# A weight product of 128 matmuls rebuilt from 28 half products, with two steps of the order moved

## The chip, the cores and the metric

The kernel runs on one core of one Trainium2 chip. The metric is the device time of a whole execution in microseconds (us). Over three runs the kernel before took 1076.21 us in the median, 1075.88 to 1081.52 us. In this text PE is the matrix engine (TensorE), DVE is VectorE, ACT is ScalarE, POOL is GpSimd, and SP is the engine whose queue issues most plain transfers. "L709" is line 709 of the kernel before; lines of the changed kernel are named as such.

## The reference

There are N = 2708 nodes with D = 1024 features and a sparse 0/1 matrix `adj` of N x N. Everything is float32. Two layers follow each other:

```python
q, k, v = x @ Wq.T + bq, x @ Wk.T + bk, x @ Wv.T + bv
z = (q @ k.T) / sqrt(D) * adj
z = where(z == 0, -10000, z)
x = layernorm(x + relu(softmax(z, axis=1) @ v))     # layer 0
x = layernorm(x + adj @ (x @ W1) + b1)              # layer 1
```

A row of `adj` holds few ones, and more of them in the low rows. So only the scores of those neighbours are needed.

## The kernel before, in words

**Sizes.** P = 128 rows make a block; there are NB = 22 blocks. The 1024 features are DC = 8 chunks of 128, or NH = 2 halves of 512. One float32 matmul with 512 columns shows up in the profile as two records.

**Opening.** Wq and Wk are loaded and turned on PE (`flip_w`, L263; copied out of PSUM by ACT and DVE in turn at L266 and L268) into `wq_o` (four tiles) and `wk_o` (one tile). From these the kernel forms the score matrix M = Wq^T Wk (L701 to L711), so that a score is x M x^T. M has 8 row blocks (`i`) by 2 halves (`h`), 16 outputs of 128 x 512, each a sum over 8 chunks: 128 matmuls. Each output is copied from its PSUM bank by ACT (L711) into a quarter tile `m_q`. Four PSUM banks (`p_o`) serve this.

**Lists of neighbours.** Between the outputs of M the program places `list_columns` (L226 to L247), one call for each of the 22 row blocks of `adj`: ACT counts the ones of the row in two passes (L231, L232), DVE finds the positions by six `max_index` over parts of the row (L235) and sorts them into 24 keys with some small operations (L237 to L245). The row block comes by a transfer on SP's queue into one of three tiles `a`; POOL writes six small marks into the tile ahead of it (L213). Sixteen lists (EARLY) are spread evenly over M. Once nine lists are placed, `sort_begin(0)` (L605 on) makes class flags of the first eight blocks on DVE (`hot`, L626); once eleven are, `sort_end(0)` counts them with two matmuls on PE (L632, L634), DVE turns the counts into places (L638 on) and POOL scatters eight records (L659). The rows are so ordered by their number of neighbours. A scheduler lays the instructions of each engine into one queue, so where the program places a call only influences where it stands in the queue.

**Block products.** `y_block(b)` (L371 to L388) forms y = x M for one block: 16 matmuls into two banks (L378), DVE adds a row (`add`, L320) and the block goes to DRAM. The loop at L757 runs the first eight (FAMILY) of these with the last six lists between them, and calls `next(deal)` after blocks 0, 1, 3, 4 and 5 (L767). `deal` is the generator `deal_hub` (L462 on), which spreads the rows with the most neighbours ("hub": up to 80 keys in each quarter row) over 128 partitions. Its steps in turn: gather the record and the four quarter rows (L494); search 80 keys by ten pairs of 677-wide DVE operations (L503, L505) and count them (`n_q`, L508); a matmul of the counts on PE (L519) with small DVE work; place the shares with eleven small DVE operations (L531 on); a transpose. The next step, eleven gathers `found`, stands in the loop of later blocks. `row_constants` (L746) is one 1024-wide DVE operation for each block.

**Attention.** The remaining blocks' products alternate with `attend` calls: POOL gathers a block's y rows (`yg`, L435) and neighbours (`g`, L441), DVE forms scores (L917) and weighted sums (L974, L1058). A credit, an estimate of time, decides how many calls go between two PE steps. The first `yg` reads the eight stored blocks of `y_block`. Then pairs of row blocks go through Wv with seven half products (`pair_products`, L322): a 2 x 2 block scheme that takes 7 products of half depth where 8 were needed, at the price of sums and differences on DVE.

**Layer 1.** `units` (L1290) gives ten pairs of row blocks in an order written by hand. For each pair POOL gathers neighbours (`sum_rows`, L1295) three units ahead, DVE sums them (L1310), `turn1` transposes the sums on PE one unit ahead of the products (`flip` L836; for block 0 `flip_shares`, L849, which also takes the hub's sums), `work1` is again seven half products. The hub's eleven gathers are placed when i == 3 (L1377). Slots to gather per block: block 0 has 15, the hub 11, block 6 has 3, blocks 5 and 11 have 4 each.

Of the kernel before, what the change touches and what calls it, by code (L numbers as in the profile page):

```python
# [9 lines left out]
F32 = mybir.dt.float32  # L10
# [5 lines left out]
ALU = mybir.AluOpType  # L16
# [4 lines left out]
P = 128  # L21
# [3 lines left out]
HALF = 512  # L25
HUB = 32
HUB_SLOTS = 11
HUB_KEYS = 80
FAMILY = 8
# [9 lines left out]
EARLY = 16  # L39
# [41 lines left out]
def sparse_part(ctx, tc, x, xT, adj, wqT, wkT, wvT, bq, bk, bv, w1, b1, out):  # L81
    nc = tc.nc
    N, D = x.shape
    DC = D // P
    NH = D // HALF
    scale = 1.0 / math.sqrt(D)
    NB = (N + P - 1) // P
    assert NB == len(SLOTS)
    rows = [min(P, N - b * P) for b in range(NB)]
# [21 lines left out]
    with es:  # L111
# [6 lines left out]
        p_o = es.enter_context(tc.tile_pool(name="p_o", bufs=4, space=PSUM))  # L118
# [4 lines left out]
        wb = tc.alloc_tile_pool(name="wb", bufs=1)  # L123
# [102 lines left out]
        def list_columns():  # L226
            b = listed[0]
            listed[0] += 1
            n, a = rows[b], loaded[b]

            nc.scalar.activation(junk[:n], a[:n], AF.Sign, accum_out=cnt[:n, b:b + 1])  # L231
            nc.scalar.activation(junk[:n], a[:n], AF.Relu, scale=-1.0, accum_out=neg[:n, b:b + 1])  # L232
            at = lists.tile([P, RANGES, 8], U16, name="at_a", bufs=2)
            for i in range(RANGES):
                nc.vector.max_index(at[:n, i], ones[:n, :8], a[:n, cuts[i] + 8 * i:cuts[i + 1] + 8 * i + 8])  # L235
            there = lists.tile([P, RANGES, 8], F32, name="there", bufs=2)
            nc.vector.tensor_tensor(there[:n], at[:n], ends[:n], op=ALU.is_lt)  # L237
# [12 lines left out]
        bcast_rows(bq_bc, bq_sb)  # L250
        bcast_rows(bk_bc, bk_sb)
        wq_o = [wv_pool.tile([P, DC, 2 * P], F32, name=f"wq_o{q}", tag=f"v{q}") for q in range(4)]
        wk_o = wb.tile([P, DC, D], F32, name="wk_o")

        def flip_w(dst, src):

            n = 0
            for c in range(DC):
                for g in range(DC // 4):
                    tr = p_tr.tile([P, 4, P], F32, name="tr")  # L260
                    for k in range(4):
                        o = g * 4 + k
                        nc.tensor.transpose(tr[:, k, :], src(c)[:, o * P:(o + 1) * P], ident)  # L263
                    to = dst(c)[:, g * 4:g * 4 + 4, :]
# [6 lines left out]
        flip_w(lambda c: wq_o[c // 2][:, :, c % 2 * P:(c % 2 + 1) * P], lambda c: wq_i[c // 2][:, c % 2, :])  # L271
        flip_w(lambda c: wk_o[:, :, c * P:(c + 1) * P], lambda c: wk_i[:, c, :])
        load_adj()
        load_adj()
        for c in range(DC):
# [5 lines left out]
        nc.vector.scalar_tensor_tensor(junk[:, :DC], bq_sb, scale, bk_sb, op0=ALU.mult,  # L281
                                       op1=ALU.mult, accum_out=bqk)
        wk_pool.release()
        xa = tc.alloc_tile_pool(name="xa", bufs=2, side="right", reuse_waits="tile")
        xs = xa.tile([P, DC, NB], F32, name="xs", bufs=1)
        junka = xa.tile([P, P], F32, name="junka", bufs=1)
        x_last = xa.tile([P, DC, HUB], F32, name="x_last", bufs=1)
        nc.vector.memset(x_last, 0.0)
        xts = []

        def load_x():
            b = len(xts)
            if b == NB - 1:
                return
            r0, n = b * P, rows[b]
            xt = xa.tile([P, DC, P], F32, name="xt", bufs=3)
            nc.sync.dma_start(out=xt, in_=xT[:, r0:r0 + n].rearrange("(c p) n -> p c n", p=P))
            xts.append(xt)

        load_adj()  # L300
        for _ in range(3):
            load_x()
        yos = [xa.tile([P, D], F32, name=f"yo{k}", bufs=1) for k in range(3)]
# [396 lines left out]

        m_q = [[wm_pool.tile([P, DC // 2, HALF], F32, name=f"m{i}{j}", tag=f"m{2 * i + j}") for j in range(NH)]  # L701
               for i in range(2)]
        done = 0
        for i in range(DC):
            for h in range(NH):
                hs = slice(h * HALF, (h + 1) * HALF)
                po = p_o.tile([P, HALF], F32, name="po")
                for o in range(DC):
                    nc.tensor.matmul(po, wq_o[i // 2][:, o, i % 2 * P:(i % 2 + 1) * P], wk_o[:, o, hs],  # L709
                                     start=(o == 0), stop=(o == DC - 1))  # L710
                nc.scalar.copy(m_q[i // 4][h][:, i % 4], po)  # L711
                while done < EARLY * (i * NH + h + 1) // (DC * NH):
                    list_columns()
                    done += 1
                    if done == FAMILY + 1:
                        sort_begin(0)
                if not sorted_ and done > FAMILY + 2:
                    records_out(*sort_end(0), 0, FAMILY)
                    sorted_.append(0)
# [37 lines left out]
        for b in range(FAMILY):  # L757
            while done < min(NB, EARLY + 2 * (b + 1)):
                list_columns()
                done += 1  # L760
            y_block(b)
            if b == 1:
                bcast_rows(u_bc, u_col)
            if b == 2:
                load_last()
            if b in (0, 1, 3, 4, 5):
                next(deal)  # L767
            row_constants(len(c_ready))
# [518 lines left out]
        bias1 = hp.tile([P, D], F32, name="bias1", tag="bias")  # L1287
        nc.sync.dma_start(out=bias1, in_=b1.to_broadcast([P, D]))

        units = [(19, 18), (17, 16), (15, 1), (14, 2), (7, 8), (9, 3), (4, 10), (6, 0), (5, 11), (12, 13)]  # L1290
        assert sorted(last + [b for unit in units for b in unit]) == list(range(NB))
        last_norm = applied[-1]
        firsts = []
# [408 lines left out]
```

## Time and profile before

| what | value |
|---|---|
| median of the three runs | 1076.21 us |
| the profiled execution's own time | 1077.36 us |
| its span, first to last instruction | 1075.6 us |
| mean granted PE clock | 0.961 |
| POOL busy | 472.9 us (44%) |
| ACT busy | 432.8 us (40%) |
| bytes moved | 228.80 MB, mean 213 GB/s |

The profile was taken on another execution than the three timed runs; its span is 1.8 us below its own time. "Busy" is time in which an engine executes; a line of the timeline gives start, length, engine, source line, operation, tiles with shapes, how many records it joins, and in brackets the idle time ahead of it and what released it.

### The profile page before, as it was taken

What the parts mean: (1) busy time and instruction counts of PE and PEld (TensorE: products, weight loads), DVE (VectorE), ACT (ScalarE), POOL (GpSimd) and SP (SyncE); (2) the same over time, 40 slices, a digit from 0 to 9 for tenths busy, and PEclk for the clock granted to TensorE, in tenths of its full rate; (3) what the DMA queues carried; (4) which work ended last, traced back from release to release, by engine and by line L of the source; (5) the groups of instructions that cost most, each with busy time, mean ns of one, the idle gap of its engine ahead of it and who ended that gap; (6) DMA issues with size and microseconds to landing.
All of it is one profiled execution on the core that took longest, in us unless ns stands there. A gap on an engine that the chain in (4) does not pass through costs nothing.

```text
span 1075.6 us, 10690 instructions
## 1 busy us (share of the span) xinstructions
PE 981.1 (91%) x2761; PEld 464.8 (43%) x2761; DVE 821.1 (76%) x2039; ACT 432.8 (40%) x902; POOL 472.9 (44%) x520
## 2 busy tenths in 40 slices
PE   8999999598999998889999999997699899769993
PEld 6444444243444443345454444443344344334441
DVE  8999698980588987997999999544668879667332
ACT  4599896042223322332433443323222432244421
POOL 0000500025267665343665663211778678867300
PEclk9999999799999998999999999999799999979997
DMA  9698858968587767545456875226778698888601
GB/s 356 186 294 242 254 161 280 317 211 233 153 274 242 232 220 219 155 143 170 142 175 216 290 237 187 82 75 236 191 284 240 177 323 320 261 227 290 135 39 42
DMA packets 105782, 228.80 MB, mean 213 GB/s; under 512 B 22500, under 2 KB 49900, under 8 KB 105710
## 3 DMA queue, kind: packets, MB, share of 16 engines
q0 software_dynamic: 48192, 147.52, 43.8%
q1 hardware_dynamic: 57518, 80.50, 23.8%
q8 instruction: 23, 0.38, 0.1%
q14 instruction: 49, 0.40, 0.1%
HBM read 217.60 MB, written 33.68 MB: 234 GB/s over the span
## 4 chain that ended last, share of the span: by engine, by line
PE 30%; DVE 18%; issue 16%; DMA 10%; POOL 8%; ACT 1%; SPq 0%; POOLq 0%; DVEq 0%; ACTq 0%
PE po L306 24%; POOL g L441 5%; PE po L378 4%; DVE junkv L917 3%; DVE r L1310 3%; DMA g<-in_x_dram,tabs 2%; DVE r L974 2%; DMA g<-x_d,tabs 2%; DMA g<-x_d,tab_h 2%; PE tr L836 1%; DVE yo L320 1%; DVE r L1058 1%; POOL yg L435 1%; POOL xr L435 1%; DMA out_dram<-t,tabs 1%
## 5 line engine op out<-in xcount | busy, mean ns | idle before, releaser
L378 PE MATMUL po<-m,xt 128*128 128x512 f32 x672 | 297.3, 603 | 8.3 <-DVE yo L320 4.8
L378 PEld LDWEIGHTS po<-m,xt 128*128 128x128 f32 x672 | 129.4, 194 | 171.7 <-issue 163.3
L306 PE MATMUL po<-t,s_all 128*128 128x512 f32 x320 | 146.5, 601 | 9.8 <-DVE xr L320 8.4
L917 DVE SCALAR_TENSOR_TENSOR junkv<-yg,g 128x1024 uint8<-128x1024 f32 x108 | 131.7, 1220 | 26.6 <-DMA g<-in_x_dram,tabs 11.9
L441 POOL DMA_INDIRECT g<-in_x_dram,tabs x84 | 108.0, 1286 | 57.2 <-DVE r L974 16.7
L1310 DVE SCALAR_TENSOR_TENSOR r<-g,valid,r 128x1024 f32<-128x1024 f32 x77 | 98.2, 1282 | 20.9 <-DMA g<-x_d,tabs 10.2
L709 PE MATMUL po<-wk_o,wq_o 128*128 128x512 f32 x256 | 110.5, 592 | 0.0
L306 PEld LDWEIGHTS po<-t,s_all 128*128 128x128 f32 x320 | 60.6, 192 | 90.6 <-issue 71.2
L441 POOL DMA_INDIRECT g<-x_d,tabs x66 | 77.8, 1179 | 25.1 <-issue 16.5
L424 ACT ACTIVATE junka<-xt 128x128 f32<-128x128 f32 x168 | 51.7, 308 | 78.9 <-PE po L378 61.7
L235 DVE FIND_INDEX8 at_a<-ones,a 128x8 uint16<-128x83 f32 (+3 forms) x132 | 82.7, 630 | 0.0
L879 ACT ACTIVATE junks<-t,lnm 128x1024 uint8<-128x1024 f32 (+1 forms) x40 | 45.9, 1148 | 89.7 <-DVE lnm L877 89.4
L974 DVE SCALAR_TENSOR_TENSOR r<-g,pr,r 128x1024 f32<-128x1024 f32 x64 | 81.7, 1280 | 0.2
L306 PE MATMUL po<-wv,s_all 128*128 128x512 f32 x160 | 74.5, 610 | 4.0 <-DVE s_all L1097 4.0
L837 ACT COPY rT<-tr 128x512 f32<-128x512 f32 x76 | 41.0, 590 | 91.2 <-PE tr L836 89.3
L709 PEld LDWEIGHTS po<-wk_o,wq_o 128*128 128x128 f32 x256 | 48.3, 190 | 59.3 <-issue 58.6
L306 PE MATMUL po<-t,rT 128*128 128x512 f32 x160 | 73.7, 603 | 0.3 <-DVE t L320 0.3
L306 PE MATMUL po<-w,rT 128*128 128x512 f32 x160 | 72.8, 600 | 0.0
L306 PE MATMUL po<-w,s_all 128*128 128x512 f32 x160 | 72.1, 592 | 0.0
L306 PE MATMUL po<-wv,rT 128*128 128x512 f32 x160 | 70.5, 592 | 0.0
L892 ACT ACTIVATE t<-t,nmr,rstd 128x1024 f32<-128x1024 f32 (+1 forms) x40 | 49.1, 1237 | 41.7 <-DVE nmr L891 33.5
L231 ACT ACTIVATE junk<-a 128x2756 uint8<-128x2756 f32 (+1 forms) x22 | 55.0, 2500 | 9.5 <-DMA a<-in_adj_dram 4.2
(354 smaller groups left out, 1393.9 us busy)
## 6 DMA issues: line engine op xcount, KB each, us to landing
xt<-in_xT_dram SPq DMA_DIRECT2D x21, 512.0 KB
y_d<-yo SPq DMA_DIRECT2D x21, 512.0 KB
a<-in_x_dram SPq DMA_DIRECT2D x21, 512.0 KB
a<-in_adj_dram SPq DMA_DIRECT2D x21, 413.5 KB
a<-in_adj_dram SPq DMA_DIRECT2D x21, 338.5 KB
a<-in_adj_dram SPq DMA_DIRECT2D x21, 263.5 KB
wq_i<-in_wqT_dram SPq DMA_DIRECT2D x8, 512.0 KB
wk_i<-in_wkT_dram SPq DMA_DIRECT2D x8, 512.0 KB
```

The costliest lines, as they stand in the source:

```text
L231: nc.scalar.activation(junk[:n], a[:n], AF.Sign, accum_out=cnt[:n, b:b + 1])
L235: nc.vector.max_index(at[:n, i], ones[:n, :8], a[:n, cuts[i] + 8 * i:cuts[i + 1] + 8 * i + 8])
L306: put = nc.tensor.matmul(acc, a[:, k], w[:, k], start=start and k == 0, stop=stop and k == DC // 2 - 1, skip_group_check=True)
L378: put = nc.tensor.matmul(po, xts[b][:, c, :], m_q[c // 4][h][:, c % 4], start=(c == 0), stop=(c == DC - 1))
L424: put = nc.scalar.activation(junka[:, :xt.shape[2]], xt[:, c, :], AF.Copy, accum_out=xs[:, c, b:b + 1])
L441: nc.gpsimd.indirect_dma_start(out=dst[:n], out_offset=None, in_=src, in_offset=bass.IndirectOffsetOnAxis(ap=at, axis=0), bounds_check=N - ...
L709: nc.tensor.matmul(po, wq_o[i // 2][:, o, i % 2 * P:(i % 2 + 1) * P], wk_o[:, o, hs], start=(o == 0), stop=(o == DC - 1))
L879: nc.scalar.activation(junks[:n], t[:n], AF.Square, bias=nm[:n], accum_out=vs[:n])
L892: applied.append(nc.scalar.activation(t[:n], t[:n], AF.Identity, bias=nmr[:n], scale=rstd[:n]))
L917: nc.vector.scalar_tensor_tensor(junkv[:n], yg[:n, :D], scale, xg[:n], op0=ALU.mult, op1=ALU.mult, accum_out=s)
L974: nc.vector.scalar_tensor_tensor(r[:n], xg[j][:n], pr[:n, j:j + 1], r[:n], op0=ALU.mult, op1=ALU.add)
L1310: put = nc.vector.scalar_tensor_tensor(r[:n], xg[:n], ok[:n, j:j + 1], r[:n], op0=ALU.mult, op1=ALU.add)
```

## The change

Three parts. **M by pairs of row blocks.** Row blocks c and c + 4 of M are formed together by seven half products of 4 matmuls each (28 half products for the four pairs, so 112 matmuls). `wk_o` becomes four quarter tiles. DVE forms four 128 x 2048 differences of quarters and adds 12 PSUM outputs of 128 x 512 into `m_q`; POOL forms 16 sums and differences of 128 x 512 of `wq_o`. ACT still copies 16 outputs. A bank `pa` is copied in the middle of its sum and then summed on. The other products use the three banks of the transposes (`spare_bank`). The loads of x and the pool `xa` move behind M, since `xa` takes the memory that `mt` holds during M. **Hub.** `next(deal)` is called after blocks 0, 1, 4, 5, 6 instead of 0, 1, 3, 4, 5. **Layer 1.** The pair (5, 11) is now eighth and (6, 0) ninth; the hub's gathers are placed at i == 4.

```diff
-        wk_o = wb.tile([P, DC, D], F32, name="wk_o")
+        wk_o = [[wb.tile([P, DC // 2, HALF], F32, name=f"wk_o{g}{h}", bufs=1) for h in range(NH)] for g in range(DC // 4)]
...
-        xa = tc.alloc_tile_pool(name="xa", bufs=2, side="right", reuse_waits="tile")
...
+        mt = tc.alloc_tile_pool(name="mt", bufs=1, side="right", reuse_waits="tile")
...
-        done = 0
-        for i in range(DC):
-            for h in range(NH):
-                hs = slice(h * HALF, (h + 1) * HALF)
-                po = p_o.tile([P, HALF], F32, name="po")
-                for o in range(DC):
-                    nc.tensor.matmul(po, wq_o[i // 2][:, o, i % 2 * P:(i % 2 + 1) * P], wk_o[:, o, hs],
-                                     start=(o == 0), stop=(o == DC - 1))
-                nc.scalar.copy(m_q[i // 4][h][:, i % 4], po)
-                while done < EARLY * (i * NH + h + 1) // (DC * NH):
...
+        done, worked = 0, 0
+
+        def product_of_m(acc, a, w, start, stop):
+            nonlocal done, worked
+            half_products(acc, a, w, start, stop)
+            worked += 1
+            while done < EARLY * worked // (7 * DC // 2):
+                list_columns()
+                done += 1
+                if done == FAMILY + 1:
+                    sort_begin(0)
+            if not sorted_ and done > FAMILY + 2:
+                records_out(*sort_end(0), 0, FAMILY)
+                sorted_.append(0)
...
+        (w11, w12), (w21, w22) = wk_o
+        A = [[(wq_of(i)[:, :DC // 2], wq_of(i)[:, DC // 2:]) for i in (c, c + DC // 2)] for c in half]
...
+        nc.vector.tensor_sub(w12, w12, w11)
+        nc.vector.tensor_sub(m_t2, w22, w12)
+        for c in half:
+            nc.gpsimd.tensor_tensor(s_a[c], A[c][1][0], A[c][1][1], op=ALU.add)
+            nc.gpsimd.tensor_tensor(s_b[c], s_a[c], A[c][0][0], op=ALU.subtract)
+        pa = [bank() for c in half]
+        for c in half:
+            product_of_m(pa[c], A[c][0][0], w11, True, False)
+            nc.scalar.copy(m_q[0][0][:, c], pa[c])
+        for c in half:
+            pb = spare_bank()
+            product_of_m(pb, A[c][0][1], w21, True, True)
+            add(m_q[0][0][:, c], pb, m_q[0][0][:, c])
+        nc.vector.tensor_sub(w11, m_t2, w11)
+        nc.vector.tensor_sub(w21, w21, m_t2)
+        for c in half:
+            product_of_m(pa[c], s_b[c], m_t2, False, False)
+            nc.scalar.copy(m_q[0][1][:, c], pa[c])
+            nc.gpsimd.tensor_tensor(s_b[c], A[c][0][1], s_b[c], op=ALU.subtract)
+        for two in (half[:2], half[2:]):
+            pc = {}
+            for c in two:
+                pc[c] = spare_bank()
+                product_of_m(pc[c], s_a[c], w12, True, False)
+                nc.scalar.copy(m_q[1][1][:, c], pc[c])
+                nc.gpsimd.tensor_tensor(s_a[c], A[c][0][0], A[c][1][0], op=ALU.subtract)
+            for c in two:
+                product_of_m(pc[c], s_b[c], w22, False, True)
+                add(m_q[0][1][:, c], pc[c], m_q[0][1][:, c])
+            for c in two:
+                product_of_m(pa[c], s_a[c], w11, False, False)
+                add(m_q[1][1][:, c], pa[c], m_q[1][1][:, c])
+        for c in half:
+            product_of_m(pa[c], A[c][1][1], w21, False, True)
+            nc.scalar.copy(m_q[1][0][:, c], pa[c])
+        mt.release()
+        xa = tc.alloc_tile_pool(name="xa", bufs=2, side="right", reuse_waits="tile")
...
-            if b in (0, 1, 3, 4, 5):
+            if b in (0, 1, 4, 5, 6):
                 next(deal)
...
-        units = [(19, 18), (17, 16), (15, 1), (14, 2), (7, 8), (9, 3), (4, 10), (6, 0), (5, 11), (12, 13)]
+        units = [(19, 18), (17, 16), (15, 1), (14, 2), (7, 8), (9, 3), (4, 10), (5, 11), (6, 0), (12, 13)]
...
-            if i == 3:
+            if i == 4:
                 sum_rows("hub")
```

In the changed kernel's PE queue, as built, the two matmuls of the first sort stand behind 86 of the 112 matmuls of M; in the kernel before they stand behind 88 of 128. The matmul of `n_q` stands behind 80 matmuls of the block products (five blocks), in the kernel before behind 70.

More of the change, by code (lines that the diff above doesn't have):

```diff
@@ L263, in flip_w @@
                         nc.tensor.transpose(tr[:, k, :], src(c)[:, o * P:(o + 1) * P], ident)
-                    to = dst(c)[:, g * 4:g * 4 + 4, :]
+                    to = dst(c, g)
                     if n % 2:
@@ L269, in flip_w, with wq_of @@
                     n += 1
-        flip_w(lambda c: wq_o[c // 2][:, :, c % 2 * P:(c % 2 + 1) * P], lambda c: wq_i[c // 2][:, c % 2, :])
-        flip_w(lambda c: wk_o[:, :, c * P:(c + 1) * P], lambda c: wk_i[:, c, :])
+        def wq_of(i):
+            return wq_o[i // 2][:, :, i % 2 * P:(i % 2 + 1) * P]
+        flip_w(lambda c, g: wq_of(c)[:, g * 4:g * 4 + 4, :], lambda c: wq_i[c // 2][:, c % 2, :])
+        flip_w(lambda c, g: wk_o[g][c // 4][:, :, c % 4 * P:(c % 4 + 1) * P], lambda c: wk_i[:, c, :])
         load_adj()
@@ L283, in sparse_part @@
         wk_pool.release()
-        xa = tc.alloc_tile_pool(name="xa", bufs=2, side="right", reuse_waits="tile")
[L285 to L298, printed above, removed]
+        mt = tc.alloc_tile_pool(name="mt", bufs=1, side="right", reuse_waits="tile")
         load_adj()
-        for _ in range(3):
-            load_x()
-        yos = [xa.tile([P, D], F32, name=f"yo{k}", bufs=1) for k in range(3)]
         def half_products(acc, a, w, start=True, stop=True):
@@ L702, in sparse_part @@
                for i in range(2)]
-        done = 0
-        for i in range(DC):
-            for h in range(NH):
-                hs = slice(h * HALF, (h + 1) * HALF)
-                po = p_o.tile([P, HALF], F32, name="po")
-                for o in range(DC):
-                    nc.tensor.matmul(po, wq_o[i // 2][:, o, i % 2 * P:(i % 2 + 1) * P], wk_o[:, o, hs],
-                                     start=(o == 0), stop=(o == DC - 1))
-                nc.scalar.copy(m_q[i // 4][h][:, i % 4], po)
-                while done < EARLY * (i * NH + h + 1) // (DC * NH):
[L713 to L719, printed above, removed]
+        done, worked = 0, 0
@@ new lines, in product_of_m, with spare_bank @@
+        def product_of_m(acc, a, w, start, stop):
[10 more added lines that the diff above has]
+                sorted_.append(0)
+        def spare_bank():
+            return p_tr.tile([P, 4, P], F32, name="tr").rearrange("p a b -> p (a b)")
@@ new lines, in sparse_part @@
+        half = range(DC // 2)
+        (w11, w12), (w21, w22) = wk_o
+        A = [[(wq_of(i)[:, :DC // 2], wq_of(i)[:, DC // 2:]) for i in (c, c + DC // 2)] for c in half]
+        s_a, s_b = [[mt.tile([P, DC // 2, P], F32, name=f"{n}{c}") for c in half] for n in ("s_a", "s_b")]
+        m_t2 = mt.tile([P, DC // 2, HALF], F32, name="m_t2")
+        nc.vector.tensor_sub(w12, w12, w11)
[3 more added lines that the diff above has]
+            nc.gpsimd.tensor_tensor(s_b[c], s_a[c], A[c][0][0], op=ALU.subtract)
@@ new lines, in sparse_part, with load_x @@
+        for c in half:
[3 more added lines that the diff above has]
+        xa = tc.alloc_tile_pool(name="xa", bufs=2, side="right", reuse_waits="tile")
+        xs = xa.tile([P, DC, NB], F32, name="xs", bufs=1)
+        junka = xa.tile([P, P], F32, name="junka", bufs=1)
+        x_last = xa.tile([P, DC, HUB], F32, name="x_last", bufs=1)
+        nc.vector.memset(x_last, 0.0)
+        xts = []
+        def load_x():
+            b = len(xts)
+            if b == NB - 1:
+                return
+            r0, n = b * P, rows[b]
+            xt = xa.tile([P, DC, P], F32, name="xt", bufs=3)
+            nc.sync.dma_start(out=xt, in_=xT[:, r0:r0 + n].rearrange("(c p) n -> p c n", p=P))
+            xts.append(xt)
@@ L720, in sparse_part @@
+        for _ in range(3):
+            load_x()
+        yos = [xa.tile([P, D], F32, name=f"yo{k}", bufs=1) for k in range(3)]
         c_all = stat.tile([P, NB, YW - D], F32, name="c_all", bufs=1)
```

## The prediction

> **What bounds the kernel now.** I read the engine totals first, then a table of 20 us stretches, then the PE's timeline, then for each wait the timeline of the engine it waits for. The totals, and the group of M:
>
> ```profile
> PE 981.1 (91%) x2761; PEld 464.8 (43%) x2761; DVE 821.1 (76%) x2039; ACT 432.8 (40%) x902; POOL 472.9 (44%) x520
> L709 PE MATMUL po<-wk_o,wq_o 128*128 128x512 f32 x256 | 110.5, 592 | 0.0
> ```
>
> PE leads over the whole, but M is one stage. Its 256 records are 128 matmuls at 110.5/128 = 0.86 us each. The stage by stretches (stretch, sum, then busy PE, PEld, DVE, ACT, POOL, clock, DMA share, GB/s):
>
> ```profile
> 60.00:80.00 20.00, 20.00 (x48) 8.85 (x47) 19.73 (x89) 19.82 (x18) 0.83 (x18) 1.00 0.88 273
> 80.00:100.00 20.00, 20.00 (x48) 8.82 (x47) 19.80 (x117) 19.69 (x20) 1.10 (x24) 1.00 0.85 246
> 180.00:200.00 20.00, 18.42 (x43) 7.79 (x41) 20.00 (x41) 4.83 (x24) 0.00 (x0) 1.00 0.99 347
> ```
>
> PE, DVE and ACT are all full during M: the lists take DVE 4.8 us each and ACT two passes of 2.5 us each (5.3 us with their ends). From 180 us DVE alone is full. PE's timeline shows what follows:
>
> ```profile
> 101.35 0.42 PE L632 MATMUL mm<-hot,lower 128*128 128x152 f32 x2
> 101.86 34.50 PE L709 MATMUL po<-wk_o,wq_o 128*128 128x512 f32 x80
> 165.64 32.78 PE L378 MATMUL po<-m,xt 128*128 128x512 f32 x76
> 210.87 0.58 PE L519 MATMUL mm<-n_q,alike 128*128 128x1 f32 x2 [12.46 <-DVE junk_h L508]
> ```
>
> The sort's matmul has no wait: DVE had finished its `hot` at 98.2. The matmul of `n_q` waits 12.46 us for DVE's 80-key search, and the next 20 records take 11.39 us where 20 x 0.43 = 8.6 is usual, 2.8 more. On the other side stands block 7: POOL's next gather waits for its stored y.
>
> ```profile
> 277.93 0.94 POOL L435 DMA_INDIRECT yg<-y_d,tabs  x1 [17.77 <-issue]
> ```
>
> PE ends block 7 at 269.1, so y landed some 9 us later. Everything of the attention hangs on this; from 425 to 675 us DVE is about 97% busy, from 660 to 746 PE, with no slack that would swallow an earlier start. Layer 1 has one large wait:
>
> ```profile
> 951.41 0.74 PE L849 MATMUL tr<-to,r 128*128 128x96 f32 x2 [15.85 <-DVE r L1310]
> ```
>
> PE waits for block 0's sums, whose fifteen gathers stand late in POOL's queue:
>
> ```profile
> 921.88 0.99 POOL L441 DMA_INDIRECT g<-x_d,tab  x1 [0.30 <-issue]
> ...
> 943.35 0.99 POOL L441 DMA_INDIRECT g<-x_d,tab  x1 [0.30 <-issue]
> ```
>
> **What the Trainium skill says.** "TensorE: Matmul & The Clock Gate" (section "Architectural detail", queue depths) has ACT and DVE as strict FIFO; the queue orders below rest on this, and the trace agrees: the search on DVE runs in line with the 1.2 us row constants. Its Part 1 says that an idle PE falls to half clock; the 2.8 us lost after the 12.46 us wait agree, with clock 0.66 in that stretch. "GPSIMD Engine Reference" (section 3.1) gives 4497 ns on GpSimd for a float32 add of 2048 elements, 2293 on DVE; the DVE side agrees (2.28 us for the 128x2048 differences at L1196), the POOL side is shown by no row. "SBUF — State Buffer" (section "Who interferes with whom") says that a DVE operation with two SBUF inputs and a GpSimd operation that reads SBUF exclude each other; no row here shows it.
>
> **M on PE.** 16 matmuls fewer x 0.859 = 13.75 us. The half products keep their 512 columns, so the price of one stays. Against this PE now waits where a bank is copied by ACT before it is summed on: I take 2.4 us in all before the sort and 0.5 after it (bounds 0 and 6; an ACT pass ahead of a copy is 2.5 us long, but three to four banks are in turn).
>
> **M on DVE.** Four differences at 2.2 (the stride of those at L1200) and twelve PSUM adds at 0.61 (the stride of L320) make 16.1 us, in a stage where DVE is 99% full. Summing the durations of DVE's queue as built, `hot` comes at 105.3 us after; before, the same sum stood some 3.3 us ahead of the trace. Lists that start about 2.5 us later (the first difference stands ahead of list 1) make it about 111. PE reaches that matmul, behind 86 of 112, at 22.7 + 3.0 (transposes between) + 86 x 0.859 + 2.4 = 102. **So PE waits 9 us for the sort, where it had none**; behind it in PE's queue are the other 26 matmuls and all block products. They end at 111 + 0.8 + 22.3 + 0.5 = 134.6, before 136.2: of 13.75 us only 1.6 is left. After such a wait the clock may be down; I take 1.5 us of the 2.8 seen (bounds 0 and 2.8).
>
> **M on POOL.** 16 operations of 512 elements, at 4497/4 = 1.12 us each (an estimate from the skill's page): 18 us on an engine that is busy 1 us in 20 here. Eight come before their use; the other eight wait for a product, and the marks of the tiles for later lists stand behind them. I take nothing for that, bounded by rival C. The loads of x now wait for `mt`: x block 0 lands at about 126 by SP's queue and is needed at 136; nothing, with 10 us of cover.
>
> **Hub.** The DVE queue's sum up to `n_q` is the same in both (187 us): 17 more of M, but three row constants ahead instead of twelve. In the trace DVE was idle for 16.6 us between 41 and 180 us, most of it behind POOL's scatters and where ACT's lists set the pace; with more DVE work these close, and `n_q` comes at 193 to 197 instead of 210.8. PE comes to it with five whole blocks done, at 134.6 + 1.3 + 80 x 0.859 + 0.9 = 205.5. The 12.46 + 2.8 = 15.3 us go, with some 9 us to spare. The steps behind it (placing, `found` gathers until about 245) are ahead of block 7's end.
>
> **Sum for the first stage.** 1.6 + 15.3 - 1.5 = 15.4 us: block 7 ends on PE at about 253.7, and POOL's first `yg` starts at about 262.5 instead of 277.93. POOL is ready at about 255, so it still waits.
>
> **Layer 1.** With (5, 11) eighth, PE does not stand at block 0's transposes but does the seventh unit's products first, until 961. Then it needs block 0. POOL has ahead of its last gather what it had, plus eight gathers of blocks 5 and 11 at 1.3 us, two stores at 2, three row gathers at 2 and a store of the last block: about 21 us with 2 of waits, so 943.35 + 23 = 966; its sum came 8 us after the last gather, hence 972 to 974. PE waits about 11 us (bounds 6 and 18) instead of 15.85: 5 us gained (10 to -2). The hub's gathers one unit later keep the same order before block 0's and add nothing.
>
> **Total.** 15.4 + 5 = 20.4. The profiled execution took 1077.36 us with a span of 1075.6: 1057.0 after. It stood 1.15 us above the median of 1076.21, so 1055.8, forecast 1056.
>
> **Rivals.** A, more is gained: `hot` is there when PE comes (the lists' drift and offset don't arise), so M keeps 13.75 - 2.9 = 10.9, the hub 15.3, less a wait of about 1 for `n_q` at 195; layer 1 gains 10 to 15. Together 35 to 40: 1036 to 1041. For it speaks that DVE work may fill the gaps before the sort; against it, DVE had 0.2 us in 20 free there. B, DVE stays the bound: the idle 16.6 us don't close, `n_q` stays at 210.8, and PE waits 5.3 with 2.8 of slow clock: 15.4 - 8 = 7.4, plus 0 to 5 in layer 1: 1064 to 1069. C, slower: POOL's operations hold up DVE, by the port or by marks that come late (before, one such queue of scatters cost DVE 5.66 us at 120 us). Each us of delay moves `hot`, PE's wait and the end of M by one. With X us the gain is 20.4 - X; it is slower from X = 20.4, by over 0.5% from X = 26. Sixteen operations at 1.9 us each give X = 30: 1085. Against it: half of them are done before the first list. D, the first stage's gain is not passed on (the DMA, up to 347 GB/s already, carries the same bytes in 15 us less) or block 0 comes beyond 979: 1071 to 1078. That the change doesn't do what it says is no rival: the queue as built has 112 matmuls.
>
> **How the numbers follow.** 0.5% is 5.4 us, about what a measurement of this kernel can tell from none: faster below 1070.8, slower above 1081.6. Forecast (1048 to 1064) 0.50, A 0.12, B 0.16, C 0.12, D 0.10. A, B, the forecast make faster 0.76 with a little off for B's upper end; D and this 0.12; C 0.12. The range leaves out C and the far end of A: 1041 to 1073.
>
> **What would show it.** M with 224 records; a wait of about 9 us ahead of the first sort's matmul, released by DVE's `hot`; no wait at the `n_q` matmul; block 7's `yg` at about 262; POOL's sums near 1.1 us; a wait of about 11 us at the transposes of block 0 in the ninth unit. It is wrong if DVE's lists stretch behind POOL's sums, if the wait for `n_q` returns, or if the time won at 262 us is gone at 425.

## The result, and the profile after

The changed kernel takes 1078.18 us in the median of 20 runs, the kernel before 1076.76 us in 20 runs beside them. The ratio is 1.0013 with a 95% interval of 0.9995 to 1.0032: no difference that the measurement can tell. The profiled execution took 1077.33 us, its span is 1075.5 us (before 1075.6). The forecast was 1056 us, the range 1041 to 1073; the time lies above both.

First the engine totals of the page after:

```profile
PE 974.2 (91%) x2729; PEld 458.5 (43%) x2729; DVE 839.1 (78%) x2055; ACT 432.0 (40%) x902; POOL 503.6 (47%) x536
```

PE is 32 records shorter, as planned. DVE has 18.0 us more, POOL 30.7 us more. The groups by form show the sums on POOL (partitions x elements, count, busy time, mean ns of one, idle time before):

```profile
L729 POOL TENSOR_TENSOR s_b<-wq_o,s_b 128x512 f32<-128x512 f32 x4 | 7.1, 1788 | 1.6 <-PE po L291 1.6
L714 POOL TENSOR_TENSOR s_a<-wq_o 128x512 f32<-128x512 f32 x4 | 7.1, 1783 | 0.3 <-issue 0.3
L736 POOL TENSOR_TENSOR s_a<-wq_o,wq_o 128x512 f32<-128x512 f32 x4 | 5.1, 1286 | 0.0
L715 POOL TENSOR_TENSOR s_b<-s_a,wq_o 128x512 f32<-128x512 f32 x4 | 5.0, 1272 | 0.0
```

Two of the four groups have means of 1.78 us, where the same size takes 1.28 elsewhere. That is a first hint that these sums stand for something. The stretches of M, in the columns used before:

```profile
60.00:80.00 20.00, 20.00 (x48) 8.93 (x47) 20.00 (x57) 19.94 (x20) 8.27 (x23) 1.00 0.55 166
80.00:100.00 20.00, 15.92 (x37) 6.81 (x36) 20.00 (x87) 15.93 (x14) 2.41 (x26) 0.99 0.86 271
100.00:120.00 20.00, 10.09 (x19) 4.64 (x18) 18.92 (x109) 17.40 (x15) 2.55 (x14) 0.67 0.69 209
220.00:240.00 20.00, 7.81 (x23) 3.44 (x21) 13.72 (x44) 2.26 (x12) 0.00 (x0) 0.82 0.95 305
```

PE has two holes: one in M (80 to 120 us, clock 0.67 at its end) and one at 220 to 240 us. Its timeline names them:

```profile
99.03 7.11 PE L291 MATMUL tr<-wk_o,s_b 128*128 128x512 f32 x12 [4.08 <-ACT m L735]
116.06 0.88 PE L617 MATMUL mm<-hot,lower 128*128 128x152 f32 x2 [9.91 <-DVE hot L611]
...
211.64 0.28 PE L504 MATMUL mm<-n_q,alike 128*128 128x1 f32 x2
...
239.97 1.25 PE L617 MATMUL mm<-hot,lower 128*128 128x266 f32 x2 [10.55 <-DVE bad L521]
```

The wait at `n_q` is gone, as forecast. The wait for the first sort is there, as forecast. But there is a third wait, of 10.55 us, that the forecast did not have: the second sort's matmul needs the one `mm` bank, which the hub's placing holds until DVE has copied it. In front of that copy, DVE's timeline shows:

```profile
227.26 0.68 DVE L305 TENSOR_TENSOR yo<-po,y_bc 128x512 f32<-128x512 f32 x1
233.94 1.23 DVE L792 SCALAR_TENSOR_TENSOR junkc<-a,u_bc 128x1024 uint8<-128x1024 f32 x1 [6.00 <-DMA a<-in_x_dram]
...
237.81 1.23 DVE L792 SCALAR_TENSOR_TENSOR junkc<-a,u_bc 128x1024 uint8<-128x1024 f32 x1
...
239.56 0.28 DVE L519 COPY place<-mm 128x128 f32<-128x128 f32 x1
239.76 0.15 DVE L521 TENSOR_SCALAR bad<-mm 128x1 f32<-128x1 f32 x1
```

The copy of `place` stands behind four row constants, and the first of them waits for x rows from DRAM. Attention and layer 1:

```profile
280.63 0.96 POOL L420 DMA_INDIRECT yg<-y_d,tabs  x1 [4.49 <-DMA y_d<-yo]
```

```profile
987.35 0.46 PE L895 MATMUL tr<-to,r 128*128 128x96 f32 x2 [1.41 <-DVE r L1356]
```

The first `yg` starts 2.7 us later than before. The wait for block 0 is 1.41 us instead of 15.85. So the ledger of the two traces is: 2.7 us lost up to the first `yg`, 7.1 more up to the product of the mean in layer 0 (508.21 against 498.41), 10.3 in all at the first wait of layer 1 (770.92 against 760.61), and all of it won back in layer 1, where the order of units is new. The 2.7 us alone say little: the kernel before and e1 below do the same work up to there, and their first `yg` are 3.9 us apart (277.93 and 274.00). At the product of the mean these two are only 1.2 us apart (498.4 and 497.2), so the loss of 9.8 us there is well clear of that scatter.

### The profile page after: what moved, and what is told of

Same layout as the page of the kernel before. It is cut to its first block, busy times and chain, and to the rows that moved or that the text cites. A ratio compares the mean times of both kernels' runs of the same rounds, so it can differ in the third digit from the quotient of the medians.

```text
span 1075.5 us, 10670 instructions
## 1 busy us (share of the span) xinstructions
PE 974.2 (91%) x2729; PEld 458.5 (43%) x2729; DVE 839.1 (78%) x2055; ACT 432.0 (40%) x902; POOL 503.6 (47%) x536
## 4 chain that ended last, share of the span: by engine, by line
PE 22%; DVE 19%; issue 17%; DMA 16%; POOL 9%; ACT 2%; POOLq 0%; SPq 0%; DVEq 0%
PE po L291 17%; POOL g L426 5%; DMA g<-x_d,tabs 4%; DMA g<-in_x_dram,tabs 3%; DVE junkv L963 3%; PE po L363 3%; DVE r L1020 2%; DMA xr<-x_d,tabs 2%; POOL xr L420 1%; DVE at_a L235 1%; DVE yo L305 1%; DMA g<-in_x_dram,tab_h 1%; DVE r L1356 1%; DMA g<-in_x_dram,tab 1%; POOL yg L420 1%
## 5 line engine op out<-in xcount | busy, mean ns | idle before, releaser
L291 PE MATMUL po<-t,s_all 128*128 128x512 f32 x320 | 149.2, 610 | 10.6 <-DVE xr L305 8.8
L1356 DVE SCALAR_TENSOR_TENSOR r<-g,valid,r 128x1024 f32<-128x1024 f32 x77 | 98.1, 1279 | 21.1 <-DMA g<-x_d,tabs 17.2
L426 POOL DMA_INDIRECT g<-x_d,tabs x66 | 80.0, 1213 | 22.5 <-issue 16.1
L231 ACT ACTIVATE junk<-a 128x2756 uint8<-128x2756 f32 (+1 forms) x22 | 55.0, 2500 | 16.2 <-DMA a<-in_adj_dram 6.3
L869 POOL DMA_INDIRECT x_d<-t,tabs x22 | 26.4, 1201 | 73.3 <-ACT t L938 61.4
L232 ACT ACTIVATE junk<-a 128x2756 uint8<-128x2756 f32 (+1 forms) x22 | 55.0, 2498 | 0.3
```

The lines of the kernel that those rows point to most:

```text
L426: nc.gpsimd.indirect_dma_start(out=dst[:n], out_offset=None, in_=src, in_offset=bass.IndirectOffsetOnAxis(ap=at, axis=0), bounds_check=N - ...
L1356: put = nc.vector.scalar_tensor_tensor(r[:n], xg[:n], ok[:n, j:j + 1], r[:n], op0=ALU.mult, op1=ALU.add)
```

## The experiments

Each kernel was timed beside the kernel before, in 4 to 22 executions; a ratio is to that kernel, with its 95% interval. Differences between two experiments are differences of ratios, with the two half widths combined as root of squares. The instants that the arguments rest on, from the traces (us from the start of the span):

| kernel | first sort on PE | M ends on PE | last list on DVE | `n_q` on DVE | `place` copied | first `yg` |
|---|---|---|---|---|---|---|
| before | 101.4 | 136.2 | 168.6 | 210.6 | 223.4 | 277.9 |
| after | 116.1 | 141.0 | 190.2 | 206.4 | 239.6 | 280.6 |
| e1 units alone | 101.1 | 136.0 | 168.9 | 210.8 | 222.5 | 274.0 |
| e2 hub alone | 101.3 | 136.2 | 169.5 | 211.5 | 234.2 | 281.9 |
| e3 M alone | 116.5 | 140.9 | 189.8 | 206.1 | 225.1 | 275.4 |
| e4 M and units | 116.7 | 142.1 | 192.8 | 209.0 | 228.1 | 278.8 |
| e5 e4 without POOL's sums | 107.0 | 131.4 | 177.1 | 194.7 | 214.9 | 264.9 |
| e6 e4 without DVE's additions | 112.1 | 142.9 | 188.0 | 204.3 | 223.3 | 274.2 |
| e7 e4 with nothing added off PE | 98.0 | 127.7 | 171.8 | 193.3 | 211.6 | 264.1 |
| e8 e4, POOL's sums on DVE | 118.0 | 130.7 | 182.0 | 199.0 | 216.7 | 265.5 |
| e10 e8 and hub | 116.0 | 128.7 | 180.1 | 197.1 | 228.6 | 269.0 |
| e14 e1 and sums beside it | 101.0 | 135.9 | 172.5 | 214.4 | 227.6 | 277.3 |

### The three parts, each alone (e1 to e4)

**e1: the order of layer 1 alone.**

```diff
-        units = [(19, 18), (17, 16), (15, 1), (14, 2), (7, 8), (9, 3), (4, 10), (6, 0), (5, 11), (12, 13)]
+        units = [(19, 18), (17, 16), (15, 1), (14, 2), (7, 8), (9, 3), (4, 10), (5, 11), (6, 0), (12, 13)]
...
-            if i == 3:
+            if i == 4:
```

> The kernel before with the layer-1 order of the change alone: (5, 11) eighth, (6, 0) ninth, the hub's gathers one unit later. DVE theory (the first stage of the changed kernel gives back on DVE what it saves on PE, and layer 1 pays for the loss in the attention): the 15.85 us wait at block 0's transposes shrinks to 1 to 3 us, 10 to 13 us faster than before (about 1065). Theory of the prediction: POOL keeps block 0 late, a wait of about 11 us stays, 5 us faster (about 1071).

1067.78 us against 1077.47, ratio 0.9909 (0.9876 to 0.9942): about 10 us faster. POOL's last gather for block 0 and PE's arrival, in e1's timelines:

```profile
966.77 1.49 POOL L441 DMA_INDIRECT g<-x_d,tab  x1 [0.30 <-issue]
```

```profile
961.74 6.25 PE L306 MATMUL po<-w,rT 128*128 128x512 f32 x14
967.83 3.60 PE L306 MATMUL po<-w,s_all 128*128 128x512 f32 x8
971.27 1.88 PE L306 MATMUL po<-w,rT 128*128 128x512 f32 x4
974.55 0.46 PE L849 MATMUL tr<-to,r 128*128 128x96 f32 x2 [1.40 <-DVE r L1310]
```

Block 0 is as late as was worked out (last gather 966.8, sums at 974.5). What was wrong is that PE has nothing else to do: 28 matmul records of the next products (the 26 in these lines and two just before), some 12 us, stand in PE's queue ahead of block 0's transposes.

**e2: the hub's steps alone.**

```diff
-            if b in (0, 1, 3, 4, 5):
+            if b in (0, 1, 4, 5, 6):
```

> The kernel before with the hub's steps moved alone. DVE theory: the wait at the n_q matmul goes, but DVE's queue and the x rows that it waits for are as late as before, so that the next step of the hub makes PE wait; within 3 us of before (1074 to 1079). Theory of the prediction: the 12.46 us wait and the 2.8 us of slow clock go and nothing takes their place: 10 to 15 us faster (1061 to 1066).

1085.43 us, ratio 1.0065 (1.0040 to 1.0090): 7 us slower, worse than either theory had it. PE's waits in e2:

```profile
211.79 0.59 PE L519 MATMUL mm<-n_q,alike 128*128 128x1 f32 x2 [4.84 <-DVE junk_h L508]
...
234.61 0.72 PE L632 MATMUL mm<-hot,lower 128*128 128x266 f32 x2 [2.74 <-DVE bad L536]
```

The two waits sum to 7.6 us instead of 12.46, so PE gained there. But `place` is copied 10.8 us later than before (234.2), POOL's last gather of `found` starts at 257.3 instead of 246.3, the first `yg` comes 4 us later (no more than the scatter named above), and PE's waits for DVE's additions of y rise from 4.8 to 17.2 us over the run.

**e3: the new M alone; e4: the new M with the order of units.** e3 is the changed kernel with the hub's steps and the units put back, e4 has the hub's steps alone put back:

```diff
-            if b in (0, 1, 4, 5, 6):
+            if b in (0, 1, 3, 4, 5):
```

> The kernel before with the new product of M alone. DVE theory: M ends on PE some 5 us later than before in spite of 16 matmuls fewer, the hub's wait stays at 3 to 8 us, and the attention starts later: 4 to 10 us slower (1080 to 1086). Theory of the prediction: 1 to 2 us faster (1075), and no more, since n_q stays where it is.

> The changed kernel with the hub's steps put back to 0, 1, 3, 4, 5. DVE theory: the hub's move is worth little either way, so 1072 to 1082, near the changed kernel (1078). Theory of the prediction: the n_q wait is back, 10 to 15 us slower than the changed kernel (1088 to 1093).

e3: 1084.18 us, ratio 1.0061 (1.0037 to 1.0084), 6.6 us slower, as the DVE theory had it; M ends on PE at 140.9 instead of 136.2. e4: 1073.26 us, ratio 0.9947 (0.9924 to 0.9969), so 4 us (plus or minus 4) more than e1, within the DVE theory's range. The changed kernel is e4 and the hub's move: 1.0013 - 0.9947 = 0.0066, 7 us (plus or minus 3). So of the three parts two cost time and one pays for both: -10 (units), +4 to +7 (M; the 4, from e4 and e1, is no larger than its uncertainty), +7 (hub).

### What the new M costs (e5 to e8, e14)

e5 to e8 start from e4, e14 from e1. e5 leaves POOL's sums out:

```diff
-        for c in half:
-            nc.gpsimd.tensor_tensor(s_a[c], A[c][1][0], A[c][1][1], op=ALU.add)
-            nc.gpsimd.tensor_tensor(s_b[c], s_a[c], A[c][0][0], op=ALU.subtract)
+        s_a, s_b = [A[c][1][0] for c in half], [A[c][0][0] for c in half]
...
-            nc.gpsimd.tensor_tensor(s_b[c], A[c][0][1], s_b[c], op=ALU.subtract)
...
-                nc.gpsimd.tensor_tensor(s_a[c], A[c][0][0], A[c][1][0], op=ALU.subtract)
```

> M by half products with the layer-1 order (hub's steps as before), the sixteen POOL sums left out: the products take the operands themselves, so M has wrong values and the rest of the work is unchanged. Theory of the lock (POOL's sums hold DVE's two-input operations up by about 9.5 us in all): the first sort's flags are ready 8 to 10 us earlier than with the sums (about 107), PE's wait there falls to 0 to 2 us, the last list comes 8 to 10 us earlier; total 3 to 6 us less than with the sums (1067 to 1070). Theory that only the number of DVE's own operations counts: nothing changes, 1073.

1057.64 us, ratio 0.9840 (0.9796 to 0.9885): 11.5 us (plus or minus 5) less than e4. The sort comes 9.7 us earlier, as the lock has it:

```profile
107.01 0.85 PE L617 MATMUL mm<-hot,lower 128*128 128x152 f32 x2 [6.28 <-DVE few L241]
```

The total fell by more than was expected, and PE's wait by less. The last list comes 15.7 us earlier, 6 more than the lock explains; over 4 of these 6 are idle time, for between 30 us and `n_q` DVE stands idle for 5.6 us here and for 10.0 us in e4.

e6 leaves out the twelve additions:

```diff
-            add(m_q[0][0][:, c], pb, m_q[0][0][:, c])
...
-                add(m_q[0][1][:, c], pc[c], m_q[0][1][:, c])
...
-                add(m_q[1][1][:, c], pa[c], m_q[1][1][:, c])
```

> The same kernel with POOL's sums kept and DVE's twelve additions into M left out (M has wrong values). DVE theory: 12 x 0.61 = 7.3 us less on DVE before the first sort, PE's wait there 8.6 - 6 = 2 to 3 us; the last list about 7 us earlier; total 2 to 5 us less (1068 to 1071). Theory that PE's waits for bank copies are what costs: the wait for the copy before the sort stays and the total changes by less than 2 us.

1069.13 us, ratio 0.9950 (0.9910 to 0.9990): not to be told from e4. PE's wait at the sort was 16.39 us, not 2 to 3: without the additions PE has no bank to wait for and comes there after 80 matmuls instead of 86. In its trace sort, `n_q` and first `yg` are each some 4.6 us earlier; the timing is too coarse to show what of that arrives.

e7 leaves out sums and additions as in e5 and e6, and the differences:

```diff
-        nc.vector.tensor_sub(w12, w12, w11)
-        nc.vector.tensor_sub(m_t2, w22, w12)
+        m_t2 = w22
...
-        nc.vector.tensor_sub(w11, m_t2, w11)
-        nc.vector.tensor_sub(w21, w21, m_t2)
```

> The same kernel with everything off PE that the new M adds left out: no POOL sums, no DVE differences, no DVE additions; 112 matmuls and 16 ACT copies stay (M has wrong values). Theory that DVE's lists and the hub's search set the end of the first stage: M ends on PE some 14 us earlier than in the kernel before, and PE waits that much longer, about 25 us, at the n_q matmul; within 3 us of the layer-1 order alone (1065 to 1070). Theory of the prediction (PE's time is on the path once nothing is added on DVE): 10 to 13 us less than that, 1055 to 1058.

1058.31 us, ratio 0.9833 (0.9799 to 0.9867): 8 us (plus or minus 5) less than e1, between the two theories. M ends on PE at 127.7, and the wait goes where it was before:

```profile
97.97 0.50 PE L617 MATMUL mm<-hot,lower 128*128 128x152 f32 x2 [2.28 <-DVE few L240]
...
193.58 0.59 PE L504 MATMUL mm<-n_q,alike 128*128 128x1 f32 x2 [8.79 <-DVE junk_h L493]
```

So the half products themselves are worth 8 us, if all that they ask of the other engines were free; DVE's `n_q`, at 193.3, is where the forecast had put it. The theory that DVE alone sets the first stage falls in this form. Next to e5 (0.9840) nothing is gained: once POOL's sums are gone, DVE's differences and additions cost no more than the timing can tell (1 us, plus or minus 6).

e8 moves the sixteen sums to DVE, four lines of this kind:

```diff
-            nc.gpsimd.tensor_tensor(s_a[c], A[c][1][0], A[c][1][1], op=ALU.add)
+            nc.vector.tensor_tensor(s_a[c], A[c][1][0], A[c][1][1], op=ALU.add)
```

> M by half products with the layer-1 order, POOL's sixteen sums moved to DVE, at 0.6 us each 9.8 us more on its queue. Theory of the lock: DVE loses about as much to POOL's sums as it would need for them itself, so flags, last list and total stay within 3 us of the kernel with POOL's sums (1071 to 1077). Theory that POOL's sums cost DVE nothing: flags and last list 10 us later, total 4 to 8 us more (1078 to 1081).

1063.49 us, ratio 0.9885 (0.9849 to 0.9921): 7 us (plus or minus 5) less than with POOL, though DVE has sixteen operations more, and the last list 11 us earlier. Neither theory had that. It is not DVE's own time: the sixteen sums take it some 0.6 us each, 9.8 us, and the lock costs it about 9 in e4. It is idle time: between 30 us and `n_q` DVE stands idle for 10.0 us in e4 and for 0.8 us in e8. The longest piece in e4 is a wait for POOL's mark for one of the lists, which stands in POOL's queue behind the scatters and reads of the first sort:

```profile
153.19 0.09 DVE L235 MATCH_VALUE_LOAD at_a<-ones,a 128x8 f32 x1 [6.10 <-POOL a L213]
```

The engine of the sums is not all that differs: in e8 as built the sort's matmuls stand behind 98 of the 112 matmuls of M, in e4 behind 86. How much of the 7 us is due to either was not taken apart; e11 below moves the sort alone, to 108, and gains nothing clear. The lock itself is seen where, in the timelines of the changed kernel, POOL's first sums and DVE meet:

```profile
43.27 4.56 POOL L714 TENSOR_TENSOR s_a<-wq_o 128x512 f32<-128x512 f32 x2 [0.32 <-issue]
47.79 2.50 POOL L715 TENSOR_TENSOR s_b<-s_a,wq_o 128x512 f32<-128x512 f32 x2
```

```profile
43.46 3.24 DVE L712 TENSOR_TENSOR m_t<-wk_o,wk_o 128x2048 f32<-128x2048 f32 x1
...
47.82 1.30 DVE L240 TENSOR_TENSOR few<-at_a,base 128x48 f32<-128x48 uint16 x1
...
49.27 1.09 DVE L241 TENSOR_TENSOR few<-few,there 128x48 f32<-128x48 f32 x1
...
51.30 0.66 DVE L305 TENSOR_TENSOR m<-tr,m 128x512 f32<-128x512 f32 x1
```

The first sum starts at 43.27; the difference on DVE starts at 43.46, and takes 3.24 us instead of 2.28: it stands until the sum is done. Then POOL's second sum stands for the difference, which is why two sums take 4.56 us instead of 2.5. The `few` operations, 0.20 us elsewhere, take 1.30 and 1.09. The addition at 51.30, which reads PSUM and one SBUF operand, runs beside a sum at its usual 0.66. Ten DVE operations of the stage are stretched so, by about 9 us in all; the kernels before and e8 have none. This agrees with the Trainium skill: "SBUF — State Buffer", section "Who interferes with whom", says that a DVE instruction with two SBUF inputs contends with a GpSimd instruction that reads SBUF, and calls the ports that they share an exclusive lock.

e14 puts sixteen idle sums beside the old M of e1, one after each output, into a buffer not yet in use:

```diff
-                    nc.tensor.matmul(po, wq_o[i // 2][:, o, i % 2 * P:(i % 2 + 1) * P], wk_o[:, o, hs],
+                    put = nc.tensor.matmul(po, wq_o[i // 2][:, o, i % 2 * P:(i % 2 + 1) * P], wk_o[:, o, hs],
...
+                w_ = wq_o[i // 2][:, :, i % 2 * P:(i % 2 + 1) * P]
+                follow(nc.gpsimd.tensor_tensor(spare, w_[:, :DC // 2], w_[:, DC // 2:], op=ALU.add), put)
```

> The kernel of e1 with M as before, and sixteen idle sums on POOL of the size that the new M uses, one released by each of M's sixteen outputs and written to a buffer that is not in use yet; nothing reads them. Theory of the lock: DVE operations with two inputs from SBUF stand while a sum runs, 0.5 to 1.1 us for each sum that meets one, 6 to 10 us in all by the trace; the list of nine comes later, PE waits up to 6 us at the first sort, n_q comes 5 to 9 us later, total 4 to 9 us more than e1 (1072 to 1077). Theory that POOL's sums cost only where something waits for their result: within 2 us of e1 (1066 to 1070).

1071.80 us, ratio 0.9977 (0.9961 to 0.9992): 7 us (plus or minus 4) more than e1. Only five DVE operations were held by a sum there, 4.6 us in all, so the first sort did not wait, against what was expected; `n_q` came 3.6 us later:

```profile
136.19 1.28 POOL L714 TENSOR_TENSOR yo<-wq_o 128x512 f32<-128x512 f32 x1
```

```profile
136.18 1.38 DVE L241 TENSOR_TENSOR few<-few,there 128x48 f32<-128x48 f32 x1
```

The sums stood ahead of other work in POOL's queue too, so that not all of the 7 us need be the lock.

### The hub's move (e9, e10)

e9 gives the second sort's first matmul another bank, in the changed kernel.

```diff
-            before = p_mm.tile([P, HALF], F32, name="mm")
+            before = p_tr.tile([P, 4, P], F32, name="tr").rearrange("p a b -> p (a b)") if f else p_mm.tile([P, HALF], F32, name="mm")
```

> The changed kernel with the second sort's first matmul writing to one of the three transpose banks instead of the single bank that the hub's place matmul still holds. Theory of the hub (the copy of place on DVE stands behind row constants that wait for x rows, and PE stands for the bank): the 10.55 us wait goes, PE comes to the transpose of row at about 244, where DVE has row at about 250, and waits 5 to 7 us there; block 7 ends 4 us earlier, total 2 to 5 us less than the changed kernel (1073 to 1076). Rival, the wait is covered by POOL's late gathers of found: within 1.5 us of it (1077 to 1080).

1073.36 us, ratio 0.9987 (0.9963 to 1.0011): 3 us (plus or minus 3) less than the changed kernel, no more than a hint. The wait goes one step on, as expected:

```profile
250.98 0.45 PE L555 MATMUL tr<-ident,row 128*128 128x128 f32 x1 [7.14 <-DVE row L548]
```

So the bank alone is not the cause. That the late copy of `place` is rests on the traces, where the hub's later steps follow it; no run moved that copy by itself. The rival of this run holds in part: in its trace the first `yg` no longer waits for block 7, but follows POOL's gathers, among them the late ones of `found`, with no more than the usual 0.30 us between:

```profile
277.10 0.96 POOL L420 DMA_INDIRECT yg<-y_d,tabs  x1 [0.30 <-issue]
```

e10 is e8 with the hub's move.

> The whole change, with POOL's sixteen sums on DVE instead (the kernel e8 with the hub's steps moved). Theory that the hub's move costs by itself: the placing comes a block later and waits for DVE, 3 to 7 us more than e8 (1066 to 1071). Theory that the move only fails where DVE is late: 1061 to 1064, no more than e8.

1070.81 us, ratio 0.9966 (0.9946 to 0.9986): 9 us (plus or minus 4) more than e8. Here DVE is not late with `n_q` (197.1), and the move costs as much as before. In e8 `place` is copied at 216.7, in e10 at 228.6, behind the same row constants:

```profile
224.28 1.23 DVE L792 SCALAR_TENSOR_TENSOR junkc<-a,u_bc 128x1024 uint8<-128x1024 f32 x1 [5.71 <-DMA a<-in_x_dram]
...
228.62 0.28 DVE L519 COPY place<-mm 128x128 f32<-128x128 f32 x1
```

### Three that missed (e11 to e13)

e11 is e4 with the first sort's counting four lists later.

```diff
-            if not sorted_ and done > FAMILY + 2:
+            if not sorted_ and done > FAMILY + 6:
```

> M by half products with the layer-1 order, POOL's sums on POOL, and the first sort's counting four lists later, so that its matmul stands behind 108 of 112 matmuls. Theory that PE's wait is handed on by ACT's queue (copies of M wait for PE, lists 15 to 17 stand behind them): PE's wait of 8.6 us goes, M ends near 133 instead of 142, the last list and n_q come 5 to 10 us earlier, total 3 to 6 us less than 1073 (1067 to 1070). Theory that the lock on DVE alone is what costs: n_q stays at 209 within 2 us, and so does the total (1071 to 1075).

1071.18 us, ratio 0.9964 (0.9944 to 0.9984), as e4. List 15 starts on ACT 6 us earlier, but the last list is at 190.3 and `n_q` at 206.6, little changed, and PE now waits a little further on:

```profile
140.94 0.58 PE L772 MATMUL mm<-bqk,ones 128*128 128x1 f32 x2 [8.76 <-DVE upto L625]
```

So ACT's queue alone is not what makes the lists late. The trace shows what takes its place: the first sort's gathers on POOL now come later, and DVE stands 7.04 us for one of them (`rec_r`), so that its idle time from 30 us to `n_q` is 8.0 us against 10.0 in e4.

e12 is e8 with the work tiles laid out in another order.

```diff
-        s_a, s_b = [[mt.tile([P, DC // 2, P], F32, name=f"{n}{c}") for c in half] for n in ("s_a", "s_b")]
         m_t2 = mt.tile([P, DC // 2, HALF], F32, name="m_t2")
+        s_b, s_a = [[mt.tile([P, DC // 2, P], F32, name=f"{n}{c}") for c in half] for n in ("s_b", "s_a")]
```

> The kernel e8 (sums on DVE) with the work tiles of M laid out in another order, so that the first three x blocks get memory that is read for the last time earlier. The 8.38 us wait of PE for an x block should go. Theory that DVE's search sets the pace: PE then waits at n_q instead, 0 to 2 us less than e8 (1061 to 1064). Theory that PE's time is on the path: about 8 us less (1055).

1062.47 us, ratio 0.9886 (0.9847 to 0.9925), as e8. PE's wait for the x block stayed at 8.6 us: the memory was not what the load waited for, so this says nothing on the two theories.

e13 holds three of e1's gathers of x rows behind the second `yg`.

```diff
+                    if (b, j) in ((5, 3), (4, 0), (4, 1)):
+                        follow(last_put[0], second_yg[0], same=True)
```

> The kernel before with the layer-1 order alone (e1), and POOL's queue at the start of the attention put into the order that it has in the kernels with the new M: six gathers of x rows, two of y, three of x rows, instead of nine of x rows and then y. Theory of the order: the stretch from the first score to the mean's product grows from about 218 to 222 to 224 us, total 3 to 7 us more than e1 (1071 to 1075). Rival, the order costs nothing and the longer stretch comes from what starts late: within 2 us of e1 (1066 to 1070).

1064.89 us, ratio 0.9917 (0.9888 to 0.9947), as e1. The stretch from first score to the mean's product is 217.6 us, no longer than in e1 (218.9). The order of the gathers does not explain the longer attention.

**A version that beats both:** e1 (0.9909) and e8 (0.9885) are each some 10 to 12 us faster than both kernels; their intervals overlap. e8 is the change without the hub's move and with the sums on DVE.

## Why the prediction was wrong, step by step

Two terms of the sum carry the miss. The hub's move was to gain 15.3 us and cost 7 (plus or minus 3). POOL's sums were put at nothing and cost 11.5 (plus or minus 5, e5). Layer 1 went the other way, 10 gained instead of 5. The measured time is at the edge of what rival D had (1071 to 1078), but not for D's reasons: there was no gain at the first `yg` to be passed on.

**M on PE** held: 16 matmuls fewer, at the old price of one. The waits for banks were 4.1 us ahead of the sort, 2.4 forecast.

**M on DVE** held as a mechanism. PE waits for the sort, 9.91 us against 9, but that the numbers are so near is luck: PE comes there 4 us later than forecast, and `hot` was ready at 116 instead of 111. The 116 has POOL's hold on DVE in it; without POOL's sums the sort comes at 107.0 (e5), so DVE's own share was rather put too high. M ended at 141.0 instead of 134.6.

**M on POOL is the first step that failed.** "I take nothing for that, bounded by rival C." The sums took 1.28 us each (1.12 estimated), and held DVE for about 9 us, the first half of rival C at a third of its price of 30. Without them the sort comes at 107.0 (e5), and the total is 11.5 us less; with the same sums on DVE, and a later sort, it is 7 us less (e8). The argument against C, that half of the sums are done before the first list, was wrong as well: the first starts at 43.27, after a mark on POOL that waits for DVE until 42.68, in the midst of the lists.

**Hub is the second.** `n_q`, forecast for 193 to 197, came at 206.4 in the changed kernel, within PE's arrival (211.6), so the old wait went as forecast; without POOL's sums `n_q` is at 194.7. What failed is the sentence after it: "the steps behind it (placing, `found` gathers until about 245) are ahead of block 7's end." The move puts the copy of `place` behind row constants that wait for x rows; it came at 239.6, `found` ended at 267 and PE waited 1.64 and 10.55 us. In three pairs of kernels (e2 to before, after to e4, e10 to e8) the move cost 7 to 9 us. By which of PE's waits and POOL's later gathers these arrive at the end was not taken apart.

**The sum for the first stage.** 15.4 us were to be gained. In the kernel before, DVE adds block 7's last half at 271.03, after a wait for PE, so PE ended it near 271 and not at 269.1, as was read. In the changed kernel that addition came at 268.93, 2.1 us gained, and the store of y then took until 280.6, some 11 us instead of 6; why, was not tried.

**Propagation.** "No slack that would swallow an earlier start" is not refuted, though from 425 to 675 us DVE was busy for 236.5 of the 250 us, 95% and not 97. But the attention was no constant either: from first score to the mean's product it took 222.3 us instead of 216.1, with DVE busy for 194.9 us in both. It was 218 to 227 us in the kernels with the new M, 216 to 222 with the old, one trace each, so that the ranges overlap; without POOL's sums (e5) it was 218.5. The gathers' order is not the reason (e13); the reason stays open. It matters for M: in e3 the first `yg` comes 2.6 us earlier than before, and the mean's product 5.2 us later (503.65 against 498.41).

**Layer 1** held in sign, and was half the size. POOL was as late as worked out (966, measured 966.8 in e1), and PE was not early: it had 12 us of other products ahead in its queue. The wait left was 1.4 instead of 11 us, the gain about 10 instead of 5.

## What to carry to other kernels

Before work goes to an engine that looks idle, ask what it shares with the engine that is full: sixteen sums on POOL held DVE up for about as long as DVE would have needed to do them itself. When a step is moved away from a wait, follow every later step of it through the queues that it now enters; the next one may stand behind work that waits for a transfer. And test the parts of a change one by one: here the new order in layer 1 alone carried a gain of 10 us, which the other two parts spent.

## What the runs showed of the hardware

In these traces a DVE operation with two operands in SBUF and a POOL sum of two SBUF operands did not run together, and each was seen to stand for the other, however small: 128x48 took up to 1.38 us instead of 0.20 on DVE (e14), and two sums took 4.56 us instead of 2.50 on POOL. A one-operand TENSOR_SCALAR of 128x8 was held as well: 0.89 us in the changed kernel, where the same operation took 0.16 us in the kernel before, and up to 1.24 us in e14. FIND_INDEX8, MAX8, MATCH_REPLACE8 and the additions that read PSUM kept their times beside POOL's sums.
